# Two transformer blocks on one core: block 0's slots taken two at a time, its norms moved earlier, and block 1's last value products moved between the scores

## The chip, the cores and the metric

The kernel runs on one core of one Trainium2 chip. Its time is the device time of one launch in microseconds. All arithmetic is in float32. A core has a matrix engine (PE, with its weight loads PEld), a vector engine (DVE), a scalar engine (ACT), GpSimd (POOL) and a queue that issues DMAs (SP). Each engine works through its own list of instructions in order and waits on semaphores for the others.

## The reference, cut to what matters

A batch has 8 sequences of 512 rows and 256 columns. Two transformer blocks follow each other. Block 0 (heads of 16 columns) is

```
h = modulate(ln(x), shift_sa, scale_sa)
q, k, v = ln(heads(h))*qn_w+qn_b, ln(heads(h))*kn_w+kn_b, heads(h)   # 16 heads, 16 columns each
x = x + gate_sa * unheads(softmax(q k^T / 4) v)                      # self-attention, 512 x 512
h = modulate(ln(x), shift_ca, scale_ca)
x = x + gate_ca * (attention(h wq, kv wk, kv wv) @ ca_out_w.T + b)   # cross-attention, 64 keys
h = modulate(ln(x), shift_ff, scale_ff)
x = x + gate_ff * ((silu(h w1) * (h w3)) @ w2)                       # feed-forward, 1024 wide
```

Block 1 (heads of 64 columns, rotary positions) has self-attention, cross-attention on the same 64 context rows and a GELU feed-forward. Rows of different sequences never meet, so the eight sequences can be at different stages at one time.

## The kernel before, in words

**Everything stays on the chip.** The rows of all eight sequences (`xs[b]`) lie in the on-chip memory from start to end. The order of instructions on PE, DVE, ACT and POOL is written out by hand: inside `manual_schedule` each engine gets its instructions in the order in which the Python code emits them. DMAs go out from SP.

**Block 0 is a row of slots.** A cycle has 18 slots (`CYCLE`); sequence `b` does self-attention in cycle `b`, cross-attention in cycle `b + 1` and the feed-forward in cycle `b + 2`. So in a cycle three sequences are at work. A slot holds at most one attention block:

- a *score* part: PE multiplies keys with queries for four heads into two PSUM tiles `ps_S` of two banks each, and ACT takes the exponential of each tile into `p` (line L574, or L696 in cross-attention). There are only two such tiles, so the next score part waits until both exponentials are done;
- a *value* part: PE multiplies `p` with the values into the bank `ps_O`. In a cross-attention block it does that and also sums `p`, into two general banks.

Sixteen slots of a cycle are self-attention (four groups `g` of four heads, four key tiles `kt` each); the slots `X0` and `X1` are the two cross-attention blocks of the sequence before. A third kind of work, *others*, is put beside the slots with `at(slot, fn)`: norms, transposes, projections, the feed-forward. Functions for the same slot run in the order of their `at` calls: first all of `batch1` (self-attention) by sequence, then the keys of block 1 (`keys1`), then for each sequence `batch2` (cross-attention) and `batch3` (feed-forward). `later` holds calls that come last in their slot.

**`run_blocks` orders a slot.** It emits the scores of slot `i`, then the values of slot `i - 1`, then the others of slot `i`.

**Names that matter below.**

- `norm(n)`, n = 0 to 2: the row norm before self-attention, in pieces: statistics of row tiles 0 and 1, of tiles 2 and 3 with the power -1/2 on POOL (L175), and the application (L208), after which POOL scales and shifts.
- `head_centre`, `head_var`, `head_scale`: the norm of each head, for halves `c` of the columns; `head_scale` has the long power on POOL (L545).
- `queries_keys(g)`: four transposes (L554), then ACT makes `q` (L557) and DVE `k` (L558).
- `group_end(g)`, `group_back(g)`: the attention result leaves `ps_O` (L587), is transposed back (L596), divided by its sums (L601 to L603), and after the last group gated and added to `xs[b]` on POOL (L608, L609).
- in `batch2` and `batch3`, `prepare(n)` is the same three pieces of a norm into `z`, a buffer that both share; `turn` transposes `z` (L416) into `hT` (L417); `queries(c)` and `up(f)` multiply `hT` with weights; `down(t)` multiplies the hidden layer with `w_2` for one tile of 128 rows and, every second tile, `add_gated` takes two tiles out of PSUM (L460, L462).
- `bank_x()` hands out three general PSUM banks in turn (names `ps_X`, `ps_X`, `ps_D`).

**Block 1's self-attention** has its own slots of two blocks: scores of an odd block `i`, other jobs, scores of `i + 1`, values of `i - 1`, values of `i`. For its last sequence there are few other jobs left.

Of the kernel before, what the change touches and what calls it, by code (L numbers as in the profile page):

```python
# [22 lines left out]
DX = D + HD0  # L23
NPAIR = H // 2
# [19 lines left out]
class Block:  # L44


    def __init__(self, scores, values):
        self.scores, self.values = scores, values
        self.before, self.after = [], []


def run_blocks(blocks, beside=None):


    beside = dict(beside or {})
    for fn in beside.pop(-1, []):
        fn()
    early, late = {}, {}
    for i, bl in enumerate(blocks):
        for lead, fn in bl.before:  # L60
            early.setdefault(max(i - lead, 0), []).append(fn)
        for lag, fn in bl.after:
            late.setdefault(i + 1 + lag, []).append(fn)
    i = 0
    while i <= len(blocks) or any(k >= i for k in (*late, *beside)):
        for fn in early.get(i, []):
            fn()
        if i < len(blocks):
            for fn in blocks[i].scores:
                fn()  # L70
        if 1 <= i <= len(blocks):
            for fn in blocks[i - 1].values:
                fn()
        for fn in (*late.get(i, []), *beside.get(i, [])):
            fn()
        i += 1


def fast_path(ctx: ExitStack, tc: tile.TileContext, a: dict, out: bass.AP):
# [150 lines left out]

    sp_stack = ExitStack()
# [56 lines left out]
    nc.gpsimd.memset(hs[0][:, :, :, HD0 : HD0 + 1], 1.0)  # L288
    nc.gpsimd.memset(sc32, 0.0)
# [189 lines left out]
    X0, X1 = 9, 13  # L479


    def batch1(b):
# [8 lines left out]
        def norm(n):  # L491

            if n == 0:
                s["bc"] = bc = wk.tile([P, 3 * D], F32, tag="bc", name="bc")
                s["h"] = hs[b % 2]
                s["hv"] = s["h"][:, :, :, 0:HD0]
                s["ln"] = wk.tile([P, NT, D], F32, tag="ln", name="ln", bufs=1)
                s["pieces"] = norm_pieces(lambda: s["ln"], xs[b], EPS0)
                if b:
                    spread(bc, b, SH_SA, 3 * D)  # L500
            s["pieces"][n]()
            if b and n == 2:
                ln, bc = s["ln"], s["bc"]
                nc.gpsimd.tensor_tensor(ln, ln, bc[:, None, D : 2 * D].to_broadcast([P, NT, D]), ALU.mult)
                shift = bc[:, 0:D].rearrange("p (h d) -> p h d", d=HD0)
                nc.gpsimd.tensor_tensor(s["hv"], ln.rearrange("p t (h d) -> p t h d", d=HD0),
                                        shift[:, None].to_broadcast([P, NT, H, HD0]), ALU.add)
# [11 lines left out]
        def head_rows():  # L519
            s["z"] = wk.tile([P, NT, DX], F32, tag="zx", name="zx", bufs=1)  # L520
            nc.gpsimd.memset(s["z"][:, :, D if b else 0 : DX], 0.0)

        def head_centre(c, par=None):

            hv = s["hv"][:, :, 8 * c : 8 * c + 8] if par is None else s["hv"][:, :, 8 * c + par : 8 * c + 8 : 2]
            sh = [P, NT, hv.shape[2]]
            mean = small.tile(sh, F32, tag=f"mean{sh[2]}", name="mean", bufs=2)
            nc.vector.tensor_reduce(mean, hv, AX.X, ALU.add)
            nc.vector.tensor_scalar_mul(mean, mean, 1.0 / HD0)
            nc.vector.tensor_tensor(parts(s["z"][:, :, 0:D], c, par), hv,  # L530
                                    mean[:, :, :, None].to_broadcast([*sh, HD0]), ALU.subtract)

        def head_var(c, par=None):
            sq, z = parts(s["ln"], c, par), parts(s["z"][:, :, 0:D], c, par)
            sh = [P, NT, z.shape[2]]
            nc.scalar.activation(sq, z, AF.Square)
            s["var", c, par] = var = small.tile(sh, F32, tag=f"var{sh[2]}", name="var", bufs=2)
            nc.vector.tensor_reduce(var, sq, AX.X, ALU.add)
            nc.vector.tensor_scalar(var, var, 1.0 / HD0, EPS0, ALU.mult, ALU.add)

        def head_scale(c, par=None, eng=None):
            var, z = s["var", c, par], parts(s["z"][:, :, 0:D], c, par)
            n = z.shape[2]
            half = mhalf[:, 0 : NT * n].rearrange("p (t h) -> p t h", t=NT)
            nc.gpsimd.tensor_tensor(var, var, half, ALU.pow)  # L545
            (eng or nc.gpsimd).tensor_tensor(z, z, var[:, :, :, None].to_broadcast([P, NT, n, HD0]), ALU.mult)

        def queries_keys(g):
# [3 lines left out]
            lo = c * P + par * HD0  # L552
            for t in range(NT):
                nc.tensor.transpose(ps[:, t * P : (t + 1) * P], s["z"][:, t, lo : lo + P], ident)  # L554
# [6 lines left out]
        def block(g, kt):  # L561
# [4 lines left out]
            def score():  # L566
# [5 lines left out]
                for u in range(2):  # L572
                    pr[u] = wk.tile([P, 2, N], F32, tag="p", name="p", bufs=4)
# [11 lines left out]
        def group_end(g):  # L585
            oT = wk.tile([P, N], F32, tag="oT", name="oT")
# [3 lines left out]
        def group_back(g):  # L590
            c, par = divmod(g, 2)
            if g == 0:
                s["attn"] = wk.tile([P, NT, D], F32, tag="tok", name="attn", bufs=1)
# [3 lines left out]
            o = s["attn"][:, :, c * P : (c + 1) * P].rearrange("p t (j e d) -> p t j e d", j=4, e=2)[:, :, :, par, :]  # L597
# [5 lines left out]
            nc.vector.tensor_tensor(o, i[:, :, :, 0:HD0], inv[:, :, :, None].to_broadcast([P, NT, 4, HD0]), ALU.mult)  # L603
            check(inv.rearrange("p t j -> p (t j)"))
            if g == 3:
                at_, x = s["attn"], xs[b]
                gate = s["bc"][:, None, 2 * D : 3 * D].to_broadcast([P, NT, D])
                nc.gpsimd.tensor_tensor(at_, at_, gate, ALU.mult)  # L608
                nc.gpsimd.tensor_tensor(x, x, at_, ALU.add)  # L609

        n = 0
        for g in range(4):
            for kt in range(NT):
# [4 lines left out]
                if g == 0 and kt == 0:  # L618
                    if b == 0:
                        def before():  # L620
                            head_rows()
# [3 lines left out]
                            first_modulated(0, 0)  # L625
                            head_centre(0, 0)
                            head_var(0, 0)
                            head_scale(0, 0, nc.vector)

                        def gate():  # L630
                            spread(s["bc"][:, 2 * D : 3 * D], b, G_SA, D)
# [3 lines left out]
                        at(0, lambda: first_modulated(0, 1))  # L635
                        at(0, lambda: head_centre(0, 1))
                        at(1, lambda: head_var(0, 1))
                        at(1, lambda: head_scale(0, 1))
                        at(2, lambda: first_modulated(1))
                        at(3, lambda: head_centre(1))  # L640
                        at(4, lambda: head_var(1))
                        at(4, lambda: head_scale(1))
                        at(5, gate)
                    else:
                        for m in range(3):
                            at(i - 11 + m, lambda m=m: norm(m))
                        at(i - 6, head_rows)
                        for c in range(2):
                            at(i - 6, lambda c=c: head_centre(c))
                            at(i - 5, lambda c=c: head_var(c))  # L650
                            at(i - 4, lambda c=c: head_scale(c))
                if kt == 0:
                    at(i - 2, lambda g=g: queries_keys(g))
                if kt == NT - 1:
                    at(i + 1, lambda g=g: group_end(g))
                    at(i + 2, lambda g=g: group_back(g))
# [3 lines left out]
    def batch2(b):  # L660
# [27 lines left out]
        def block(c):  # L688
            def score():
# [4 lines left out]
                for u in range(2):  # L694
                    s["p", c, u] = p = wk.tile([P, 2, N], F32, tag="p", name="p", bufs=4)
# [35 lines left out]
        for n in range(3):  # L731
            at(base + 3 + n, lambda n=n: prepare(n))
# [12 lines left out]
    def batch3(b):  # L745
        s = {}

        base = CYCLE * (b + 2) + (3 if b in (B - 3, B - 2) else -2 if b == B - 1 else 0)
# [28 lines left out]
        def down(t):  # L777
            qp, j = divmod(t, 2)
            if j == 0:
                s["ps"] = bank_x()  # L780
            project_tile(s["ps"], j, lambda k: s["hid"][:, k, :], w_2, 8, t)
            if j == 1:
                add_gated(wk2, b, s["gate"])(qp, s["ps"].rearrange("p (j d) -> p j d", j=2))

        for n, i in enumerate((5, 5, 5) if b == B - 1 else (4, 5, 7)):
            at(base + i, lambda n=n: prepare(n))
        later.append((base + 7, turn))
        for f in range(8):
            at(base + 8 + f, lambda f=f: up(f))
        for t in range(4):  # L790
            at(base + 16 + t, lambda t=t: down(t))
# [58 lines left out]
    def keys1(p):  # L850
# [3 lines left out]
        kv1[p] = q = kv1["pool"].tile([P, N], F32, tag="q", name="q", bufs=5)  # L854
# [47 lines left out]
    for p in range(NPAIR):  # L902
        at(CYCLE + 4 + p, lambda p=p: keys1(p))
        at(CYCLE + 8 + p, lambda p=p: store_keys1(p))
# [10 lines left out]
    run_blocks(blocks, beside)  # L915
# [37 lines left out]
    with tc.tile_pool(name="ph4", bufs=2) as wk:  # L953
# [171 lines left out]
        def slots():  # L1125
            n = B * NG * NT
            for m in range(-1, n // 2):

                i = 2 * m + 1
                if i >= 0:  # L1130
                    todo[i // 16][0](i % 16 // NT, i % NT)
                jobs = steps.get(m, [])[:]
                if m in mid:
                    jobs.insert(1, mid[m])
                for fn in jobs:
# [3 lines left out]
                for k in (i - 1, i):  # L1139
# [1108 lines left out]
```

## The time and the profile before

| | |
|---|---|
| median of 3 runs | 2444.23 us (2443.59 to 2446.45) |
| the profiled execution: its own time | 2446.33 us |
| its span, first to last instruction | 2444.5 us |
| block 0: first scores to the first projections of block 1 | about 20 to 865 us |
| a full cycle (cycles 3 to 6) | 97.67 us each |
| after the last value part of cycle 7 | 731 to 865 us, feed-forward and cross-attention of the last sequences |
| block 1's self-attention, its cross-attention and feed-forward | to about 1838 us, to the end |
| PE busy, DVE, ACT, POOL | 98%, 47%, 36%, 39% of the span |

The page gives the busy time of each engine, the span in 40 slices, the DMA queues, the chain that ended last and the costliest groups. The timeline lists instructions in order of time, with neighbours of one kind merged. A merged row has its start, its length, the engine, the line, what it writes and reads, the rows and columns of the PE array and the number of instructions. A float32 matrix product appears as two instructions. The length of a PE row includes a modelled end, so distances between starts are the better measure.

### The profile page before, as it was taken

How to read it: one execution, taken by the hardware profiler on the slowest of the kernel's cores; microseconds unless marked ns; L12 is line 12 of the kernel's file. 1: busy time of each engine (PE TensorE's matmuls, PEld its weight loads, DVE VectorE, ACT ScalarE, POOL GpSimd, SP SyncE). 2: the span in 40 equal slices, each digit the busy share in tenths (PEclk: the TensorE clock that was granted, in tenths of full speed). 3: DMA queues.
4: the chain of work that ended last, by engine and by line, in shares of the span. 5: the costliest groups of instructions: out<-in, count | busy, mean ns of one | idle time of the engine just before them, and what ended most of it. 6: DMA issues, size and time to landing. Idle time of an engine off the chain costs nothing.

```text
span 2444.5 us, 28454 instructions
## 1 busy us (share of the span) xinstructions
PE 2400.8 (98%) x10964; PEld 1144.0 (47%) x10964; DVE 1147.0 (47%) x2083; ACT 887.0 (36%) x1118; POOL 955.7 (39%) x538
## 2 busy tenths in 40 slices
PE   9999999999998999999999999999999999999998
PEld 4333443444435543444444444444435555567665
DVE  4554435434434436464646454545444756651210
ACT  4565545545452123333333333333332221222221
POOL 3543222322301036555555555555543544531110
PEclk9999999999999999999999999999999999999999
DMA  5120000000001100000000000000123222210000
GB/s 181 45 93 7 16 20 8 17 11 12 13 11 55 36 1 23 19 19 19 19 18 19 18 19 18 19 18 19 36 60 98 67 68 67 63 55 27 22 18 23
DMA packets 84400, 84.07 MB, mean 34 GB/s; under 512 B 42544, under 2 KB 58784, under 8 KB 84256
## 3 DMA queue, kind: packets, MB, share of 16 engines
q1 hardware_dynamic: 83352, 81.09, 10.6%
q8 instruction: 88, 1.44, 0.2%
q10 hardware_dynamic: 904, 1.07, 0.2%
q14 instruction: 56, 0.46, 0.1%
HBM read 72.09 MB, written 10.04 MB: 34 GB/s over the span
## 4 chain that ended last, share of the span: by engine, by line
PE 88%; DVE 4%; POOL 3%; issue 2%; DMA 1%; ACT 1%; SPq 1%; POOLq 0%; DVEq 0%; ACTq 0%
PE ps_X L109 37%; PE ps_S L109 22%; PE ps_D L109 13%; PE ps_O L109 13%; PE ps_X L416 1%; DMA rb<-rec 1%; POOL x L437 1%; DMA rec<-rec 1%; DVE t L836 1%; POOL p L1260 1%; POOL q L991 1%; POOL oT L1073 1%; ACT p L574 0%; SPq L1253 0%; PE ps_X L554 0%
## 5 line engine op out<-in xcount | busy, mean ns | idle before, releaser
L109 PE MATMUL ps_S<-q,k 32*128 32x512 f32 (+1 forms) x3072 | 423.6, 624 | 8.1 <-ACT p L574 3.1
L1008 ACT ACTIVATE p<-ps_S 128x1024 f32<-128x1024 f32 x256 | 250.6, 1022 | 461.8 <-PE ps_S L109 452.0
L574 ACT ACTIVATE p<-ps_S 128x1024 f32<-128x1024 f32 x256 | 248.1, 1021 | 231.9 <-PE ps_S L109 230.5
L109 PEld LDWEIGHTS ps_S<-q,k 32*128 32x128 f32 (+1 forms) x3072 | 142.4, 184 | 242.0 <-issue 170.2
L1027 DVE TENSOR_TENSOR sm<-sm,p 128x1024 f32<-128x1024 f32 x128 | 253.2, 2037 | 2.2 <-ACT p L1008 2.2
L987 DVE TENSOR_TENSOR t<-ps_X,rope_c 128x512 f32<-128x512 f32 x126 | 87.0, 690 | 340.9 <-PE ps_X L109 340.9
L175 POOL TENSOR_TENSOR rstd<-rstd,mhalf 128x4 f32<-128x4 f32 x49 | 51.1, 1042 | 325.6 <-DVE rstd L174 324.8
L990 POOL TENSOR_TENSOR q<-t 128x512 f32<-128x512 f32 x32 | 65.5, 2047 | 288.3 <-DVE t L988 288.3
L837 POOL TENSOR_TENSOR q<-t,t 128x512 f32<-128x512 f32 x72 | 94.5, 1312 | 176.4 <-DVE t L836 170.2
L109 PE MATMUL ps_X<-hT,w 128*128 128x512 f32 x344 | 160.5, 601 | 1.4 <-ACT hT L417 0.9
L1023 POOL TENSOR_TENSOR sm<-p 128x1024 f32<-128x1024 f32 x64 | 149.9, 2369 | 3.6 <-ACT p L1008 3.6
L109 PE MATMUL ps_O<-p,h 128*32 128x512 f32 x1024 | 138.9, 613 | 1.6 <-ACT oT L587 1.6
L1073 POOL TENSOR_TENSOR oT<-oT,rb 128x512 f32<-128x512 f32 x63 | 130.8, 2093 | 18.1 <-DMA rb<-rec_d 18.1
L109 PE MATMUL ps_O<-p,v 128*64 128x512 f32 x512 | 134.8, 605 | 0.0
L109 PE MATMUL ps_D<-p,v 128*64 128x512 f32 x512 | 131.6, 592 | 0.0
L109 PE MATMUL ps_X<-w_sa_wv,hT 128*128 128x512 f32 x256 | 118.0, 604 | 0.0
L990 POOL TENSOR_TENSOR k<-t 128x512 f32<-128x512 f32 x32 | 40.8, 1275 | 194.7 <-DVE t L988 187.5
L545 POOL TENSOR_TENSOR var<-var,mhalf 128x32 f32<-128x32 f32 (+1 forms) x17 | 87.3, 5133 | 75.5 <-ACT t L773 41.7
L109 PE MATMUL ps_X<-hT,w_sa_wq 128*128 128x512 f32 x256 | 115.9, 595 | 0.0
L109 PE MATMUL ps_X<-w_sa_wo,oT 128*128 128x256 f32 x512 | 114.5, 382 | 0.1
L109 PE MATMUL ps_X<-hT,w_sa_wk 128*128 128x512 f32 x248 | 114.6, 605 | 0.0
L109 PE MATMUL ps_S<-hT,w_ff_w 128*128 128x512 f32 x256 | 111.3, 593 | 0.0
(282 smaller groups left out, 3589.3 us busy)
## 6 DMA issues: line engine op xcount, KB each, us to landing
rb<-rec SPq DMA_DIRECT2D x128, 128.0 KB
rb<-rec_d SPq DMA_DIRECT2D x124, 128.0 KB
rb<-rec SPq DMA_DIRECT2D x16, 256.0 KB
out_dram<-x SPq DMA_DIRECT2D x15, 256.0 KB
x<-in_x_dram SPq DMA_DIRECT2D x7, 512.0 KB
bc<-modd SPq DMA_DIRECT2D x7, 384.0 KB
gate<-modd SPq DMA_DIRECT2D x16, 128.0 KB
k_d<-q SPq DMA_DIRECT2D x8, 256.0 KB
```

The source lines that it names most:

```text
L109: nc.tensor.matmul(o, lhsT, rhs, start=start, stop=stop)
L175: nc.gpsimd.tensor_tensor(r[:, :n], r[:, :n], mhalf[:, :n], ALU.pow)
L416: nc.tensor.transpose(ps[:, t * P : (t + 1) * P], z[:, t, k * P : (k + 1) * P], ident)
L545: nc.gpsimd.tensor_tensor(var, var, half, ALU.pow)
L574: nc.scalar.activation(pr[u], pss[u], AF.Exp, scale=HD0 ** -0.5)
L837: nc.gpsimd.tensor_tensor(dst, t1, t2, ALU.add)
L987: nc.vector.tensor_tensor(c, ps, rope_c, ALU.mult)
L990: nc.gpsimd.tensor_tensor(r[0], ec, os, ALU.subtract)
L1008: nc.scalar.activation(pr, pss[u], AF.Exp, scale=HD1 ** -0.5)
L1023: nc.gpsimd.tensor_tensor(sm, s["p", g, 0, u], s["p", g, 1, u], ALU.add)
L1027: nc.vector.tensor_tensor(s["sm", g, u], s["sm", g, u], s["p", g, t, u], ALU.add)
L1073: eng.tensor_tensor(o, o, s["rb", g, u], ALU.mult)
```

## The change

Block 0 from slot 18 on is emitted in groups of two slots. For odd `i` the order becomes: scores of `i`, others of `i - 2`, others of `i - 1`, scores of `i + 1`, values of `i - 1`, values of `i`. The first cycle keeps the old order. With that:

- `X0` moves from slot 9 to 11, so that a group of heads ends in an odd slot or ahead of a cross-attention block;
- `queries_keys` comes four slots ahead of its scores and not two; `norm` of the next sequence comes at 13, 12 and 10 slots ahead (before: 11, 10, 9), behind cross-attention's first two norm pieces; the head norms are spread over slots -9 to -3;
- the head norms write into two kept tiles `zs[c]` (set to zero once) in place of one tile per sequence;
- each group is gated and added to `xs[b]` by itself, in place of all four at the end; `gate` and `bc` are separate DMAs;
- cross-attention's `prepare` comes in slots 3, 3, 5 (before 3, 4, 5; the last sequence 3, 3, 4); the feed-forward's in 4, 4, 7 (before 4, 5, 7), `turn` in 8, `up` from 9, `down` in every second slot from 17 for sequences 0 to 5; each `down` has a PSUM bank and two DVE instructions of its own;
- the key projections of block 1 in cycle 1 are spread over 12 slots; `p` has six buffers in place of four, other buffers have fewer.

In the last three slots of block 1's self-attention, the values of block `i - 1` come between the two score parts.

```diff
-    while i <= len(blocks) or any(k >= i for k in (*late, *beside)):
...
+    others(-1)
+    for i in range(alone):
+        scores(i)
+        values(i - 1)
+        others(i)
+    scores(alone)
+    values(alone - 1)
+    for i in range(alone + 1, max(len(blocks) + 2, *(k + 3 for k in beside)), 2):
+        scores(i)
+        if i > alone + 1:
+            others(i - 2)
+        others(i - 1)
+        scores(i + 1)
+        values(i - 1)
+        values(i)
...
-    X0, X1 = 9, 13
+    X0, X1 = 11, 13
...
+            x, gate = (v.rearrange("p t (h d) -> p t h d", d=HD0)[:, :, 8 * c + par : 8 * c + 8 : 2]
+                       for v in (xs[b], s["gate"][:, None, :]))
...
-            if g == 3:
-                at_, x = s["attn"], xs[b]
-                gate = s["bc"][:, None, 2 * D : 3 * D].to_broadcast([P, NT, D])
-                nc.gpsimd.tensor_tensor(at_, at_, gate, ALU.mult)
-                nc.gpsimd.tensor_tensor(x, x, at_, ALU.add)
+            nc.gpsimd.tensor_tensor(attn, attn, gate.to_broadcast([P, NT, 4, HD0]), ALU.mult)
+            nc.gpsimd.tensor_tensor(x, x, attn, ALU.add)
...
-                        for m in range(3):
-                            at(i - 11 + m, lambda m=m: norm(m))
-                        at(i - 6, head_rows)
+                        for m, k in enumerate((-11, -10, -9) if b == 1 else (-13, -12, -10)):
+                            at(i + k, lambda m=m: norm(m))
                         for c in range(2):
-                            at(i - 6, lambda c=c: head_centre(c))
-                            at(i - 5, lambda c=c: head_var(c))
-                            at(i - 4, lambda c=c: head_scale(c))
+                            for k, fn in zip((-6, -5, -5, -4) if b == 1 else (-7, -5, -3, -3) if c else (-9, -8, -7, -7),
+                                             (head_centre, head_square, head_var, head_scale)):
+                                at(i + k, lambda c=c, fn=fn: fn(c))
                 if kt == 0:
-                    at(i - 2, lambda g=g: queries_keys(g))
+                    at(i - (2 if i <= CYCLE else 4), lambda g=g: queries_keys(g))
                 if kt == NT - 1:
                     at(i + 1, lambda g=g: group_end(g))
-                    at(i + 2, lambda g=g: group_back(g))
+                    at(i + 2 + (b > 0 and n % 2 == 0), lambda g=g: group_back(g))
...
-        for n in range(3):
-            at(base + 3 + n, lambda n=n: prepare(n))
+        for n, i in enumerate((3, 3, 4 if b == B - 1 else 5)):
+            at(base + i, lambda n=n: prepare(n))
...
-        base = CYCLE * (b + 2) + (3 if b in (B - 3, B - 2) else -2 if b == B - 1 else 0)
+        base = CYCLE * (b + 2) + {B - 3: 4, B - 2: 3, B - 1: -2}.get(b, 0)
...
+            ps = bank_x()[:, 0:D]
+            project_tile(ps, 0, lambda k: s["hid"][:, k, :], w_2, 8, t)
+            tmp = wk2.tile([P, 2, D], F32, tag="tmp", name="tmp", bufs=1)[:, 0, :]
+            nc.vector.tensor_tensor(tmp, ps, s["gate"], ALU.mult)
+            x = xs[b][:, t, :]
+            nc.vector.tensor_tensor(x, x, tmp, ALU.add)
+
+        places = {B - 2: (3, 3, 5, 6, 8), B - 1: (5, 5, 5, 7, 8)}.get(b, (4, 4, 7, 8, 9))
...
-            at(base + 8 + f, lambda f=f: up(f))
+            at(base + places[4] + f, lambda f=f: up(f))
         for t in range(4):
-            at(base + 16 + t, lambda t=t: down(t))
+            at(base + places[4] + 8 + (t if b > B - 3 else 2 * t), lambda t=t: down(t))
...
-        at(CYCLE + 4 + p, lambda p=p: keys1(p))
-        at(CYCLE + 8 + p, lambda p=p: store_keys1(p))
+        at(CYCLE + 4 + 5 * p // 3, lambda p=p: keys1(p))
+        at(CYCLE + 7 + 5 * p // 3, lambda p=p: store_keys1(p))
...
+                end = m > n // 2 - 4
...
+                if end:
+                    todo[-1][1](2 * m % 16 // NT, 2 * m % NT)
                 for fn in jobs:
                     fn()
                 if i + 1 < n:
                     todo[(i + 1) // 16][0]((i + 1) % 16 // NT, (i + 1) % NT)
-                for k in (i - 1, i):
+                for k in (i - 1, i)[end:]:
```

## The prediction

> **What bounds the kernel now.** I read the page first: the engines' shares and the chain that ended last.
>
> ```profile
> PE 2400.8 (98%) x10964; PEld 1144.0 (47%) x10964; DVE 1147.0 (47%) x2083; ACT 887.0 (36%) x1118; POOL 955.7 (39%) x538
> ...
> PE 88%; DVE 4%; POOL 3%; issue 2%; DMA 1%; ACT 1%; SPq 1%; POOLq 0%; DVEq 0%; ACTq 0%
> ```
>
> PE is the bound, so the change can only pay in what PE loses between products. For that I read PE's timeline by starts: a dense slot first, then two slots without other work on PE.
>
> ```profile
> 405.60 1.14 PE L109 MATMUL ps_S<-q,k 16*128 16x512 f32 x8
> 406.67 1.06 PE L109 MATMUL ps_O<-p,h 128*32 128x512 f32 x8
> 407.66 1.98 PE L109 MATMUL ps_X<-hT,w 128*128 128x512 f32 x4
> 409.48 1.88 PE L109 MATMUL ps_D<-hT,w 128*128 128x512 f32 x4
> 411.29 1.14 PE L109 MATMUL ps_S<-q,k 16*128 16x512 f32 x8
> ...
> 465.88 1.14 PE L109 MATMUL ps_S<-q,k 16*128 16x512 f32 x8
> 466.95 1.06 PE L109 MATMUL ps_O<-p,h 128*32 128x512 f32 x8
> 468.19 2.04 PE L109 MATMUL ps_S<-q,k 16*128 16x512 f32 x8 [0.17 <-ACT p L574]
> 470.16 1.07 PE L109 MATMUL ps_O<-p,h 128*32 128x512 f32 x8
> 471.16 1.39 PE L109 MATMUL ps_S<-q,k 16*128 16x512 f32 x8
> ```
>
> Scores take 1.07 us, values 1.00, the eight products of an `up` 3.63, though single ones follow each other every 0.429 (8 x 0.429 = 3.43): 0.20 goes to the changes of shape. Start by start a change costs about 0.1 on each side: after values the first full product starts 0.543 later, not 0.43; scores' second group 0.534 behind the first. Within one shape 0.43 holds. In the second stretch the scores wait for the exponentials: their first half starts 1.24 after the values' start, their second 0.92 later, at **2.155**.
>
> [...] DVE's timeline has the program's order:
>
> ```profile
> 376.49 0.17 DVE L601 COPY den<-ps_D 128x16 f32<-128x16 f32 x1 [3.87 <-PE ps_D L596]
> 376.70 0.25 DVE L602 RECIPROCAL inv<-den 128x16 f32<-128x16 f32 x1
> 376.99 0.42 DVE L603 TENSOR_TENSOR attn<-ps_D,inv 128x256 f32<-128x256 f32 x1
> 377.33 0.23 DVE L146 TENSOR_REDUCE chk<-inv 128x1 f32<-128x16 f32 x2
> 377.48 0.74 DVE L199 BATCH_NORM_STATS2 st<-x 128x6 f32<-128x256 f32 x2
> ...
> 378.55 1.37 DVE L208 TENSOR_SCALAR z<-x,mv,rstd 128x256 f32<-128x256 f32 x4
> ```
>
> `group_back` (1.0), statistics (0.95), application (1.37): z is ready 4.1 us after the slot's transposes began, and the transposes of `turn` wait for it, here 0.4.
>
> **Part 1, groups of two slots (gain).** Old, two dense slots: 2 x (1.07 + 1.00 + 0.20) + F, F the other products. New: two scores 2.14, others F + 0.20, two value parts in one shape 0.454 + 2 x 0.43 + 0.543 = 1.86: 4.20 + F. That saves 0.34. But the values' 1.86 must cover the exponentials' 2.155, so the second half of the next scores comes 0.30 late, except behind the two cross-attention blocks, whose values are 0.855 longer. F of the nine pairs in a full cycle, from 0.109 a transpose, 0.429 and 0.216 a product of 512 and 256: 3.9, 7.35, 3.9, 4.8, 4.3, 7.7, 6.9, 7.3, 7.3 = 53.4. All exceed the 2.2 that cover the exponentials of the first scores, so no light slots remain. A cycle: 9 x 4.20 + 53.4 + 1.71 + 7 x 0.30 = **95.0**, against 97.67 measured (of which 1.7 is waiting of the light slots): 2.65 less.
>
> **Part 2, what is late next (loss).** Others of slots 5 and 6 now follow each other with nothing between. PE: `group_back`, the last `down`, `turn`. DVE, in `at` order: `group_back`, the next norm's statistics, the two instructions that take `down` out of PSUM, only then cross-attention's `prepare(2)`, whose z `turn` needs. From the last product of `down`: 0.42 until DVE starts (as L460 does), 0.45 and 0.35 for the two (L603's 0.424 for 256 columns from PSUM, half of L462's 0.69), 1.37 for z, 0.6 for the remaining transposes: 3.2, against 1.15 without a wait. PE stalls **2.0** in cycles 3 to 7. In cycle 2, without a `down`, z is ready at 4.3, `turn` could begin at 0.6: 3.4 of stall. In cycle 1 key rotations (2.1 of DVE) stand ahead too: 3.8. Behind PE's wait are queued the scores of `i + 1`, both value parts and, through the exponentials, ACT.
>
> **Sum by stretches**, slot for slot at equal work.
> - Cycle 1 (71.55): fewer changes, `queries_keys` earlier (scores waited 1.6 for L558 once), but light pairs and the 3.8: 0.8 less.
> - Cycle 2 (95.55): same sums with 3.4: 1.6 less.
> - Cycles 3 to 6: 97.67 - 95.0 - 2.05 = 0.6 each, 2.5.
> - Cycle 7 and the tail to 865: PE needs some 120 of the tail's 134, so 13 is waiting, 4.7 of it one gap before L416 at 752. With `down` of sequence 5 in slots 3, 5, 7, 9 that gap shrinks to about 2.2 (statistics 1.9, power 1.25 and z behind a `down` eviction, against one `down` of 3.45 on PE). But pairs of slots 9 to 12 in cycle 7 have F of 0.9 (1.07 late each), and `turn` in slot 23 waits 2.1, since per-tile evictions put the norm behind a `down`: 4.4 less.
> - Block 1's last three slots: the row for 16 scores and 32 scores there shows waits of 2.35 and 0.9 for exponentials; 1.87 of values between covers most, but the last sums wait for DVE's additions (two of them 3.44): 1.6 less.
>
> Total 10.9 less. **The clock takes some back**: nine stalls of 2 us and more[...]. By the phase of the window I count the two long ones and one of the rest: three windows at half speed, 1.7 each, 5.1 more. In all -5.8, rounded to **-6**.
>
> **Costed at nothing.** POOL: two instructions of 2.35 per sequence become eight of 256 columns, about 0.6 each (L546's 256 columns: 0.617), 5.0 for 4.7, with POOL 39% busy; if it were late, the next norm would be. DVE gets 4 x 0.8 for 2 x 1.4 per `down` set. The long power (5.43) begins three slots earlier and `queries_keys` two, with 7 us or more between; in cycle 1 I allow 0.5. `queries_keys` only needs the two `q` and `k` buffers whose scores are over. SP: one more DMA of 128 KB per sequence (`gate`), issued in 0.3 with slots to spare; key stores are later by up to 5 slots, feed-forward weights then land some 10 us later, with over 25 left before `up`. Zeroing `zs` takes about the 0.99 that L521 took at 2.5 us; POOL is next needed at 7.3. Six `p` buffers are what three blocks in flight need. If one of these covers fails, it adds to the loss side only; together I bound them by 0 and 8 us.
>
> **Profiled and plain time.** The sum is made against the profiled execution (span 2444.5, own time 2446.33), 2.1 above the median. I apply the difference to the median: 2444.2 - 6 = 2438.
>
> **The rivals.**
> - *The stall is not there*, since z's pieces get ready ahead of the eviction: then 5 x 2.0 + 3.4 + 3.8 come back and no clock is lost: -28, 2416. For it: cycle 4 before has only 0.4. Against: DVE's order above.
> - *Gains and waits cancel*: DVE is slower beside POOL (z took 2.23 for four at 381.88, L462 2.15 at 362.93, against 1.37 and 0.69). With 1 us more in each of seven cycles: +1, 2445, no change to be seen.
> - *The clock decides* (slower): the wait in front of L416 in slot 6 makes a window idle enough each time, and a second follows, as here:
>
> ```profile
> 750.00:754.60 4.60, 2.68 (x13) 2.02 (x11) 1.85 (x4) 0.00 (x0) 0.00 (x0) 1.00 0.01 4
> 754.60:761.50 6.90, 4.27 (x11) 2.41 (x12) 3.24 (x12) 1.55 (x2) 4.06 (x3) 0.52 0.06 17
> ```
>
>   (window; PE, PEld, DVE, ACT and POOL busy; then the clock: 1.00, then 0.52.) Thirteen windows at 1.7 are 22, so +11, 2455. It decides from 6.4 windows on (10.9 / 1.7). [...]
> - That groups are not formed is excluded by the loop itself.
>
> **How the numbers follow.** 0.2% of 2444 is 4.9 us, about what a measurement of this kernel can tell from no change. Forecast, chance 0.50, its own range 2430 to 2443: faster 0.35, same 0.15. No stall: 0.12, faster. Cancelling: 0.17, same 0.14, slower 0.03. Clock: 0.21, slower 0.20, same 0.01. Together faster 0.47, same 0.30, slower 0.23. The range 2419 to 2456 leaves out the far ends of the first and last rival; it takes in the 8 us of covers.
>
> **What would show it.** Pairs of value parts 1.86 long followed by scores of 1.37, not 1.07. In cycles 3 to 6, a wait of PE for z (L208) of about 2 us in front of cross-attention's transposes, once a cycle, 3.4 and 3.8 in cycles 2 and 1; cycles of about 97. The gap at 752 cut to half. If cycles last 95, the stall is absent; over 98, the clock or DVE's contention is seen in PE's granted clock or in longer rows of z. Wrong as a whole if PE waits anew somewhere not listed here.

## The result and the profile after

The changed kernel takes **2467.95 us** (2466.44 to 2469.52) beside 2444.63 us: 23 us more, a ratio of 1.0095 with an interval of 1.0077 to 1.0112. The profiled execution has a span of 2464.3 us at an own time of 2466.44, so spans can be compared with each other (2464.3 against 2444.5, +19.8).

The page of the changed kernel, its line of busy times and the shares of the chain that ended last:

```profile
PE 2406.5 (98%) x10964; PEld 1163.9 (47%) x10964; DVE 1151.4 (47%) x2115; ACT 889.8 (36%) x1118; POOL 961.8 (39%) x580
...
PE 86%; DVE 4%; POOL 3%; issue 3%; DMA 1%; ACT 1%; SPq 0%; POOLq 0%; DVEq 0%; ACTq 0%
```

PE issues as many products as before and is still the bound. It is "busy" 5.7 us longer with them, so some products take longer; the timelines below show which. The stretches are read from the trace by the start of the first scores of each cycle, and by the first products of block 1:

| profiled execution, us | before | after |
|---|---|---|
| cycle 1 | 71.55 | 80.67 |
| cycle 2 | 95.54 | 100.19 |
| cycles 3, 4, 5, 6 | 97.67 each | 97.47, 100.40, 97.47, 100.40 |
| cycle 7 and the tail, to block 1 | 221.7 | 225.0 |
| block 1's self-attention | 972.8 | 970.9 |
| half clock between 85 us and the end of block 1's self-attention | 17 | 55 |

Two `down` calls (6.9 us) have moved from cycle 2 to later, so at equal work cycle 2 is 11.6 longer and the stretch of cycle 7 is 3.6 shorter.

Cycle 4 shows the wait that was forecast. PE's timeline around cross-attention's transposes (start, length, line, what it writes and reads, idle time before it):

```profile
402.33 1.30 PE L427 MATMUL ps_D<-ident,z 128*128 128x128 f32 x4 [1.30 <-DVE z L215]
...
404.27 2.09 PE L116 MATMUL ps_S<-q,k 16*128 16x512 f32 x8
406.29 3.64 PE L116 MATMUL ps_O<-p,h 128*32 128x512 f32 x16
```

and DVE's timeline for the same time:

```profile
401.07 0.42 DVE L786 TENSOR_TENSOR tmp<-ps_X,gate 128x256 f32<-128x256 f32 x1 [1.45 <-PE ps_X L116]
401.53 0.42 DVE L788 TENSOR_TENSOR x<-x,tmp 128x256 f32<-128x256 f32 x1
401.87 1.38 DVE L215 TENSOR_SCALAR z<-x,mv,rstd 128x256 f32<-128x256 f32 x4
```

DVE takes `down` out of PSUM in two instructions and only then makes z, in the order that the prediction worked out. But look at the two PE rows behind the wait: scores last 2.09, not 1.14, and sixteen value products 3.64, not 1.92. PE runs at half speed, at a granted clock of 0.50 (403.66 to 407.08 below).

From 85 us to the end of block 1's self-attention the stretches at half clock in this trace begin at 93.05, 99.88, 120.36, 181.80, 205.69, 403.66, 601.64 and 966.86 us, always a whole number of 3.413 us apart, and last one, two or three times as long. In the trace of before they begin at 157.53 and 754.86, 175 times 3.413 apart, and last 10.24 and 6.83. So a trace can be cut at these borders into windows of 3.41 us. The table (us; busy PE, PEld, DVE, ACT, POOL with counts; then the granted clock, the share of the DMA engines and GB/s) has the windows with the waits of cycles 3, 4 and 7, and the one behind cycle 4's:

```profile
301.26:304.68 3.42, 2.30 (x11) 1.69 (x9) 1.94 (x8) 0.00 (x0) 2.23 (x4) 1.00 0.00 0
400.25:403.66 3.41, 2.11 (x10) 1.13 (x9) 2.56 (x8) 0.00 (x0) 1.06 (x3) 1.00 0.10 30
403.66:407.08 3.42, 3.42 (x16) 0.99 (x18) 3.36 (x8) 2.11 (x3) 3.32 (x2) 0.50 0.05 15
697.21:700.62 3.41, 2.11 (x11) 1.53 (x9) 1.26 (x4) 0.00 (x0) 1.85 (x3) 1.00 0.00 0
```

The wait is 1.3 us each time, and PE is busy for 2.30, 2.11 and 2.11 us, but only behind cycle 4's window does the clock fall, for two windows. So busy time alone does not decide. What differs is the work: in cycles 3 and 7 the window holds 2.30 and 2.08 us of `down` products, in cycle 4 only 0.78 of them and 1.33 of transposes. The fall is the 2.93 between cycles 3 and 4. It comes again in cycle 6 (0.67 of `down`, 1.45 of transposes) and not in cycle 5 (2.19 of `down`).

Cycle 2 shows a wait that was not forecast. PE's waits between 80 and 210 us (for what, us in total, times, longest), the forecast ones for z of cycles 1 and 2 among them:

```profile
PE ps_D L116 <- DVE oT L734: 8.0, 1, 8.0
PE ps_X L427 <- DVE z L215: 7.3, 4, 3.8
```

The 8.0 us are cross-attention's output projection (`project_out`), which waits for `scaled` (L734), which waits for the DMA of `rb`. The queue of SP and POOL's and DVE's timelines say why:

```profile
175.19 0.31 SPq L865 DMA_DIRECT2D k_d<-q  x1
175.60 0.38 SPq L729 DMA_DIRECT2D rec<-rec  x1
177.27 0.39 SPq L262 DMA_DIRECT2D w<-in_w1T_dram  x1
177.76 0.62 SPq L731 DMA_DIRECT2D rb<-rec  x1
```
```profile
167.33 5.44 POOL L561 TENSOR_TENSOR var<-var,mhalf 128x32 f32<-128x32 f32 x1
...
173.87 1.29 POOL L843 TENSOR_TENSOR q<-t,t 128x512 f32<-128x512 f32 x1
```
```profile
169.72 0.34 DVE L726 RECIPROCAL rec<-rec 128x32 f32<-128x32 f32 x1
...
185.03 0.69 DVE L734 TENSOR_TENSOR oT<-oT,rb 128x512 f32<-128x512 f32 x1 [10.47 <-DMA rb<-rec]
```

The last key of block 1 is emitted behind the long power on POOL (5.44), so its sum is done at 175.2. Its store heads SP's queue, and the reciprocals, ready at 170.1, go out only at 175.60. Then their `rb` is under way for 7 us, among 3 MB of feed-forward weights, which are loaded as soon as that last store is through.

### The profile page after: what moved, and what is told of

It reads as the page before. It is cut to its first block, busy times and chain, and to the rows that moved or that the text cites. A ratio compares the mean times of both kernels' runs of the same rounds, so it can differ in the third digit from the quotient of the medians.

```text
span 2464.3 us, 28541 instructions
## 1 busy us (share of the span) xinstructions
PE 2406.5 (98%) x10964; PEld 1163.9 (47%) x10964; DVE 1151.4 (47%) x2115; ACT 889.8 (36%) x1118; POOL 961.8 (39%) x580
## 4 chain that ended last, share of the span: by engine, by line
PE 86%; DVE 4%; POOL 3%; issue 3%; DMA 1%; ACT 1%; SPq 0%; POOLq 0%; DVEq 0%; ACTq 0%
PE ps_X L116 35%; PE ps_S L116 22%; PE ps_O L116 13%; PE ps_D L116 13%; PE ps_X L427 1%; DMA rb<-rec 1%; POOL x L448 1%; DVE t L842 1%; DVE z L215 1%; POOL p L1270 1%; ACT p L590 0%; PE ps_X L610 0%; POOL q L997 0%; POOL var L561 0%; POOL oT L1079 0%
## 5 line engine op out<-in xcount | busy, mean ns | idle before, releaser
L116 PE MATMUL ps_S<-q,k 32*128 32x512 f32 (+1 forms) x3072 | 430.9, 632 | 5.6 <-ACT p L590 3.4
L116 PEld LDWEIGHTS ps_S<-q,k 32*128 32x128 f32 (+1 forms) x3072 | 149.5, 187 | 249.7 <-issue 164.5
L116 PE MATMUL ps_X<-hT,w 128*128 128x512 f32 x328 | 151.0, 597 | 0.5 <-DVE t L779 0.5
L621 POOL TENSOR_TENSOR attn<-attn,gate 128x256 f32<-128x256 f32 x32 | 23.2, 727 | 261.6 <-DVE attn L619 255.9
```

The source lines that it names most:

```text
L116: nc.tensor.matmul(o, lhsT, rhs, start=start, stop=stop)
```

## The experiments

**Theory:** the gains of groups and tail are there; the loss is (1) half clock, started by short waits, (2) the 8.0 us for `rb`, (3) the forecast waits for z. **Rivals:** groups themselves are slow where little other work lies between; the clock is a mere by-product of the waits.

| kernel | median us | ratio to the kernel before, run beside it; interval |
|---|---|---|
| changed | 2467.95 | 1.0095, 1.0077 to 1.0112 |
| e_prep | 2433.66 | 0.9951, 0.9939 to 0.9964 |
| e_fill | 2461.35 | 1.0062, 1.0047 to 1.0078 |
| e_clock | 2468.68 | 1.0085, 1.0071 to 1.0100 |
| e_clock2 | 2450.64 | 1.0022, 1.0012 to 1.0032 |
| e_keys | 2464.06 | 1.0085, 1.0062 to 1.0108 |
| e_ff | 2466.41 | 1.0077, 1.0048 to 1.0106 |
| e_k32 | 2458.47 | 1.0050, 1.0035 to 1.0065 |
| e_third | 2457.36 | 1.0049, 1.0030 to 1.0068 |
| e_nogroups | 2457.06 | 1.0048, 1.0032 to 1.0063 |
| e_b_end | 2442.32 | 0.9984, 0.9977 to 0.9992 |
| c_prep_keys | 2435.36 | 0.9970, 0.9957 to 0.9982 |
| c_prep_k32 | 2432.56 | 0.9945, 0.9930 to 0.9959 |
| c_fill | 2431.35 | 0.9941, 0.9928 to 0.9954 |
| c_hold | 2431.05 | 0.9943, 0.9929 to 0.9956 |
| c_hold_fill | 2425.14 | 0.9906, 0.9889 to 0.9922 |

Cycle lengths below come from each kernel's one profiled execution (for e_keys, c_prep_keys and c_hold their fastest, for c_hold_fill its slowest).

### The wait for z (e_prep)

```diff
-        for n, i in enumerate((3, 3, 4 if b == B - 1 else 5)):
+        for n, i in enumerate((3, 3, 4)):
```

> The changed kernel, with the third norm piece of cross-attention one slot earlier (slot 4 in place of 5 for every sequence), so that it is emitted a group ahead of its transposes. Theory (waits for z in slot 6, and half-clock windows that follow from them): waits of 1.5 in cycles 3 to 7, 3 and 3.8 in cycles 2 and 1 go, and the stretches at half clock at 120, 205, 403 and 601 us: 18 to 26 us less, 2442 to 2450; cycles 4 and 6 last as long as 3 and 5. Rival (the clock falls for another reason): 12 to 14 less, 2454 to 2456, with cycles 4 and 6 still 3 us longer. Rival (the wait only moves to another instruction of DVE): 0 to 3 less.

34 us less than the changed kernel, more than the 18 to 26 of the theory. PE's timeline at the same place of a steady cycle, and DVE's z:

```profile
375.42 3.62 PE L116 MATMUL ps_X<-w,hid 128*128 128x256 f32 x16
378.87 0.60 PE L427 MATMUL ps_D<-ident,z 128*128 128x128 f32 x4
...
379.84 1.14 PE L116 MATMUL ps_S<-q,k 16*128 16x512 f32 x8
```
```profile
375.69 1.38 DVE L215 TENSOR_SCALAR z<-x,mv,rstd 128x256 f32<-128x256 f32 x4
```

z is ready at 377.1, under `down`'s products, and the transposes follow them without a gap. Cycles 3 to 6 are 95.30 each, where the prediction's sum without a stall was 95.0. So the wait costs 97.47 - 95.30 = 2.17 a cycle, and half clock 2.93 more in every second one. Cycle 1 falls from 80.67 to 66.28: 3.8 of that is the wait there; the rest is put down to the half clock, of which none is left between 85 and 158 us. The wait for `rb` is still 6.5.

### Clock and waiting taken apart (e_fill, e_clock, e_clock2)

e_fill makes PE work while it waits for z, e_clock also in the wait for `rb` and in five pairs with little other work. e_clock2 is e_clock with products of half the width:

```diff
         def turn():
+            ps = bank_x()
+            for _ in range({0: 8, 1: 6}.get(b, 3)):
+                mm(ps[:, 0:D], ident, w_q0[:, 0, :])     # e_fill, e_clock: all 512 columns
             s["hT"] = transposed(wk2, s["z"], b, modT[:, 2:4, :], modT[:, 0:2, :])
...
+    for i in (0, 2, 16, 18, 22):
+        at(CYCLE + i, fill)                              # 3 products; not in e_fill
+    at(2 * CYCLE + 1, lambda: fill(17))                  # not in e_fill
```

> The changed kernel, with products of constants put in front of cross-attention's transposes, into a bank that nobody reads: 3 of 0.43 us where the wait is 1.5, 6 and 8 of them in cycles 2 and 1. The waits for z stay as they are, only PE is busy in them. Theory (cycles 4 and 6 lose 2.9 each to the clock, not to the wait itself): all four steady cycles last 97.5, the stretches at 120, 205, 403 and 601 us are gone, 8 to 14 us less, 2454 to 2460. Rival (the clock follows something other than PE's activity, or the added products cost time themselves): cycles 4 and 6 stay at 100.4, 2468 or more.

> The changed kernel, with all its waits left, but with products of constants in them: those before cross-attention's transposes, 17 before the first output projection of cross-attention in cycle 2 (where the wait is 8.0) and three in each of five light pairs. Theory (the clock is more than half of the loss): no half-clock time between 85 and 800 us, 2450 to 2456. Rival (the waits are the loss, the clock a small part): 2459 to 2464.

> The changed kernel, with all its waits left and with products of constants in them as in the kernel before this one, but half as wide: 3 of 0.43 us before cross-attention's transposes in cycles 3 to 7, 6 and 8 in cycles 2 and 1, 17 before the first output projection of cycle 2, three in each of five light pairs. Theory (the clock costs more than the waits): no half-clock time between 85 and 800 us, cycles 3 to 6 of 97.5 each, cycle 1 at 71 to 74, cycle 2 at 95 to 100; 2450 to 2456. Rival (what the clock gives is lost again, since the waits end at times that POOL and the DMAs set): 2459 or more.

In e_fill all four steady cycles last 97.87 to 97.88: the 2.93 is gone from cycles 4 and 6, with the wait left. The granted clock there is 1.00, for 0.97 in cycles 4 and 6 of the changed kernel, and nothing but PE's activity was added. Products of 512 columns took 0.86, though, twice what I had written (two instructions of 0.43). So e_fill has 0.41 too much in each cycle, and its 6.6 us less fall short of the 8 to 14 expected: its cycle 2 has six windows at half clock and takes 104.5. And e_clock, with 17 of them (14.6 us) in a wait of 8.0, lost again what it won: half clock gone (mean clock 0.997 for 0.987), time unchanged. By its number the theory failed there, and e_clock decides nothing. e_clock2 has the intended size. Its windows for cycles 3 and 4:

```profile
252.90:350.40 97.50, 97.23 (x511) 46.45 (x510) 45.55 (x123) 50.57 (x62) 29.83 (x20) 1.00 0.05 14
350.40:447.90 97.50, 97.23 (x511) 46.47 (x510) 43.77 (x111) 50.58 (x62) 29.81 (x20) 1.00 0.05 14
```

Both are 97.5 long at a clock of 1.00. Cycle 1 takes 73.83, cycle 2 95.82. Only one window at half clock is left between 85 us and the end of block 1's self-attention, and the median is **17.3 us below the changed kernel**, with nothing moved and no wait taken away. So half clock makes some 17 us of the changed kernel's time, and the rival that it is a by-product falls: it has a price of its own. With the waits for z (five of 2.17, 3.8 and 2.8) that makes 34.7, near the 34 of e_prep; only near, since e_prep keeps four slow windows. Not all of the 17 is new: the kernel before has 17 us at half clock itself.

### The wait for rb (e_keys, e_ff, e_k32)

```diff
-        at(CYCLE + 4 + 5 * p // 3, lambda p=p: keys1(p))
-        at(CYCLE + 7 + 5 * p // 3, lambda p=p: store_keys1(p))
+        at(CYCLE + 4 + p, lambda p=p: keys1(p))              # e_keys
+        at(CYCLE + 8 + p, lambda p=p: store_keys1(p))
+        at(CYCLE + 4 + 3 * p // 2, lambda p=p: keys1(p))     # e_k32
+        at(CYCLE + 7 + 3 * p // 2, lambda p=p: store_keys1(p))
...
-    at(2 * CYCLE, open_ff)
+    at(2 * CYCLE + 3, open_ff)                               # e_ff, with the next line in it
+            nc.vector.memset(w[:, 0, 0:1], 0.0)
```

> The changed kernel, with block 1's keys projected one slot after the other again and stored in slots 8 to 15 of cycle 1. Theory (the last store of a key stands in SP's queue ahead of cross-attention's second reciprocals, which then travel together with the feed-forward weights): the 8.0 us wait in cycle 2 goes, and with it part of the half-clock stretch at 182 us: 8 to 10 us less, 2458 to 2460. Rival (the wait is only the collision with 3 MB of weights, wherever they stand): at most 3 less, 2465 to 2468, and the wait appears at the transfer of the first head instead.

> The changed kernel, with the feed-forward weights held back (by a small memset three slots later) until cross-attention's second reciprocals are on their way; the key stores stay. Theory (two parts: 5.5 us behind the key store in SP's queue, 3.7 us of slower transfer beside the weights): the wait of 8.0 falls to 4 to 5, 3 to 4 us less, 2464. Rival (weights alone): 8 less, 2460. Rival (queue alone): no change, 2468.

> The changed kernel, with the last two keys of block 1 one and two slots earlier (keys in every slot 3p/2 in place of 5p/3), so that the last rotation's addition on POOL stands ahead of the power of 5.4 us and not behind it. Theory (the last key's store holds up SP's queue, with cross-attention's second reciprocals behind it): the wait of 8.0 us falls to 0 to 3, 5 to 9 us less, 2459 to 2463. Rival (the weights, which then start earlier too, delay rb all the same): the wait stays over 5, above 2465.

In e_k32 PE waits no more for `rb`, and the time falls by 9.5, as the theory said, but not for its reason. Cycle 1 has 6.8 of the 9.5 (73.87 for 80.67). In cycle 2, PE from the first scores to the projection, and DVE's `scaled`:

```profile
159.69 2.10 PE L116 MATMUL ps_S<-q,k 16*128 16x512 f32 x8 [0.30 <-ACT p L590]
161.72 3.51 PE L116 MATMUL ps_O<-p,h 128*32 128x512 f32 x16
...
176.12 2.25 PE L116 MATMUL ps_D<-w_o,oT 128*128 128x256 f32 x8
```
```profile
176.06 0.69 DVE L734 TENSOR_TENSOR oT<-oT,rb 128x512 f32<-128x512 f32 x1 [5.73 <-DMA rb<-rec]
```

`rb` is there 16.4 us after the cycle's first scores, in the changed kernel 18.6: 2.2 earlier. PE gets to the projection 5.8 later, since it ran at half clock on the way. The same comparison for the others (us after the first scores of cycle 2; the last two are described below):

| | `scaled` starts | first product of the projection | wait for `rb` | half clock between |
|---|---|---|---|---|
| before | 5.6 | 8.5 | 0 | 8.1 |
| changed | 18.6 | 10.7 | 8.0 | 0 |
| e_keys | 18.5 | 16.5 | 2.2 | 10.2 |
| e_ff | 16.0 | 10.7 | 5.5 | 0 |
| e_k32 | 16.4 | 16.4 | 0 | 10.2 |
| c_prep_k32 | 15.7 | 11.6 | 4.3 | 0 |
| c_hold | 9.5 | 11.6 | 0 | 0 |

In e_keys `rb` comes no earlier at all. Its shorter wait is a slow PE, and cycle 2 still takes 99.2; the median falls by 4, with an interval that overlaps the changed kernel's. In e_ff, too, the time did not move measurably. So a shorter wait in a trace is not yet a gain, and neither the store nor the weights alone bring `rb` more than about 3 us forward. These kernels vary by the clock: one execution of e_keys took 2457.85 at a mean clock of 0.990, another 2471.65 at 0.984.

### Groups or the moves around them (e_third, e_nogroups, e_b_end)

```diff
-    run_blocks(blocks, beside, CYCLE)
+    run_blocks(blocks, beside, 2 * CYCLE)         # e_third
+    run_blocks(blocks, beside, len(blocks))       # e_nogroups
```

> The changed kernel, with groups from the third cycle on (slot 36) in place of the second. Theory (in cycle 1 a group without much other work leaves PE light, and the clock falls without any long wait): cycle 1 goes from 80.7 to 71 to 73 us with no half-clock stretches between 92 and 131 us; 8 us less, 2460. Rival (what was moved in cycle 1, norms and keys, makes it longer, not the groups): cycle 1 stays at 79 to 81, 2467.

> The changed kernel with no groups at all: slots one by one to the end, everything that was moved stays moved. Theory (groups put the norm's last piece, the eviction and the transposes into one stretch, so they make the wait; by themselves they save 2.4 a cycle): no wait for z in slot 6, steady cycles of 97 to 98 all alike, cycle 1 near 71; 2446 to 2452, between the changed kernel and the one with the earlier norm piece. Rival (the moved norms and keys make the loss, the groups only gain): waits for z stay, cycles of 99 to 102, above 2468.

> The kernel before with the change to block 1's last three slots alone (values between the two score parts). Theory (the cover of exponentials by values): the last slots of block 1's self-attention 26.7 to 23.2 us, 3.6 us less, ratio 0.9985. Rival (a half-clock window follows, as at 967 us in the changed kernel): 2 us less. Rival (the sums wait for DVE all the same): no change.

e_nogroups has no wait in the steady cycles, 97.26 each: against e_prep's 95.30 a group order without its wait is worth 2.0 a cycle. But it waits 9.8 for `rb`, cycle 2 is 104.7, and the total is above the kernel before and above what I expected: that wait belongs to the moved keys, not to the groups. e_third's gain of 10.6 looks like the theory's (cycle 1 at 74.2), but nearly half of it is cycle 2 (94.5), where the wait for `rb` was only 2.2. And e_prep has cycle 1 in groups at 66.3, so groups with little between them need not be slow. But they can be: four of the seven slow windows of the changed kernel's cycle 1 (at 93.05 and from 99.88 on) follow no gap on PE longer than 0.8 us. The two windows ahead of them, 89.64 to 93.05 and 96.46 to 99.88, hold 2.54 and 2.24 us of scores, 0.66 of transposes and at most 0.35 of value products. That is what a light group puts side by side. This rival is therefore right in part: light groups cost something in the changed kernel and nothing at that place in e_prep (clock 1.00 in its cycle 1). That the place of the scores in the windows decides which is my reading; no run varied it alone. e_b_end: block 1's self-attention 969.2 for 972.8, as the theory had it, and 0.16% less in all.

### Put together (c_prep_keys, c_prep_k32, c_fill, c_hold, c_hold_fill)

c_prep_keys and c_prep_k32 are e_prep with the key places of e_keys and e_k32. c_hold is c_prep_k32 with e_ff's edit. c_fill and c_hold_fill add three products to five light pairs (`fill` above), of 512 columns in c_fill, of 256 in c_hold_fill.

> Both moves together: cross-attention's third norm piece in slot 4 for every sequence, and block 1's keys projected and stored as in the kernel before. Theory: the wait of 6.5 us for rb, left in cycle 2 by the first move alone, shrinks to 0 to 2 with the stretch at half clock behind it: cycle 2 falls from 94.6 to 85 to 88, 6 to 9 us less than the first move alone: 2425 to 2428. Rival (the second move gained only in cycle 1, where the first has already taken the loss away): no less than 2431.

> The same key places together with cross-attention's third norm piece in slot 4. Theory: the wait for rb in cycle 2 (6.5 us with the norm piece alone) goes to 0 to 2 and nothing is lost in cycle 1: 5 to 8 us less than with the norm piece alone, 2426 to 2429. Rival (the last pairs of cycle 1 and the first of cycle 2 are so light that PE's clock falls there with or without the wait): 0 to 3 less, 2431 to 2434.

> The kernel with the earlier norm piece and the earlier keys, and with the feed-forward weights loaded only once cross-attention's second rb has been used (a small memset behind it on DVE). Theory (the reciprocals' write of 16 KB waits behind 2 MB of weights): it lands in 2 us, the wait of 4.3 for rb falls to 0 to 1, cycle 2 from 91.4 to 86 to 88, 3 to 5 us less: 2427 to 2430. Rival (the first pairs of cycle 2 are light, and the clock falls there in any case): cycle 2 stays above 89, 2431 to 2433.

> The kernel just before this one, with three products of constants of 0.43 us each put into five light pairs of cycles 1 and 2 (beside slots 18, 20, 34, 36 and 40), into a bank that nobody reads. Theory (light pairs alone let the clock fall): half-clock time between 85 and 200 us is gone, 3 to 6 us less than without, 2422 to 2425, and the runs lie closer together. Rival (the products cost what they last, up to 6.4 us, and the clock falls anyway): no less than without, 2428 to 2433.

> The kernel with all three mends (norm piece, keys, weights held) and three products of constants of 0.43 us in each of five light pairs of cycles 1 and 2. Theory (in some runs the clock falls in these light pairs): every run near the fastest one of the kernel without them, 2421 to 2426, at a mean clock of 0.996 or more. Rival (the clock falls later in those runs, or the products cost their own time): median 2429 to 2433, no narrower.

The first two gave nothing that can be told from e_prep: the rivals' side. c_prep_keys pays in cycle 1 (68.96 for 66.28, a wait of 2.0 behind key rotations on DVE). In c_prep_k32 PE, now at full clock until the wait, still waits 4.3 for `rb`. SP's queue:

```profile
153.12 0.39 SPq L262 DMA_DIRECT2D w<-in_w1T_dram  x1
...
156.49 0.34 SPq L729 DMA_DIRECT2D rec<-rec  x1
...
163.47 0.62 SPq L731 DMA_DIRECT2D rb<-rec  x1
```

Now the weights go first, and the 16 KB of reciprocals take 7 us until `rb`, which waits for them, can be issued. In c_hold, where the weights come later, SP's queue and PE's projection read

```profile
156.41 0.32 SPq L729 DMA_DIRECT2D rec<-rec  x1
157.87 0.62 SPq L731 DMA_DIRECT2D rb<-rec  x1
```
```profile
163.64 1.89 PE L116 MATMUL ps_D<-w_o,oT 128*128 128x256 f32 x8
```

1.5 us for the same 16 KB, no wait, and cycle 2 takes 84.93 for 91.43. So the store ahead in the queue and the weights each hide the other: with either gone `rb` comes 2.2 to 2.9 us earlier, with both gone 9.1. In the medians, where the theory had 2427 to 2430, c_hold shows only 1.5 less than c_prep_k32, which is no measurable gain: its executions lie between 2420.27 at a clock of 0.997 and 2435.24 at 0.991, those of c_prep_k32 between 2426.98 and 2439.18. c_fill's products cost what they gave: cycle 1 is 5.1 longer than without. With half of them c_hold_fill takes **2425.14** (2420.14 to 2428.61, clocks of 0.995 to 0.998): closer together than c_hold in only four executions, 0.9% below the kernel before, 43 us below the changed one. It is the fastest of all.

## Why the prediction was wrong

It said 2438 with a range to 2456; 2468 came. Step by step:

- **Part 1 was right.** The pair model and its cycle of 95.0 met 95.30 where the wait is gone.
- **Part 2 was right in mechanism and size.** 2.17 for 2.05 in steady cycles, 3.8 for 3.8 in cycle 1, 2.8 for 3.4 in cycle 2; the cause was DVE's order as written.
- **The other sums were near.** At equal work cycle 7 and the tail gave 3.6 less (forecast 4.4), block 1's end 3.6 in e_b_end (forecast 1.6; half clock at 967 us took half of it back in the changed kernel). The gap of 4.7 at 752 us is gone; the longest wait for z behind it is 1.5 (forecast 2.2).
- **The clock was the step that failed most.** For it "three windows at half speed, 1.7 each, 5.1 more" stood in the sum, on top of the kernel before. There were 16 (55 us) where the kernel before has 5 (17 us): eleven more. The price was about right: with the new last slots, block 1's self-attention lasts 969.2 to 969.3 in the eight runs without a slow window and 970.9 to 971.0 in the eight with one; e_clock2, with fifteen fewer and products of its own, has a span 18.1 shorter, some 1.2 a window. So the term was 13 to 19 us, by my estimate from these two prices, and not 5.1. The choice of three out of nine stalls was my estimate, made at a single phase of the windows, and not shown by the trace of before. There half clock follows windows with PE busy for 1.84 us (154.12 to 157.53) and 1.23 (751.45 to 754.86), but not one with 1.84 (51.72 to 55.13). In cycle 4 of the changed kernel it followed a wait of 1.3. I had also counted PE only as busy or idle, so that the windows before 93.05 and 99.88, with PE busy for 3.40 and 2.83 us in scores, transposes and few value products, were not in the count. The rival "the clock decides" had 13 windows and the right sign; it lacked the next point.
- **A cover failed.** "Feed-forward weights then land some 10 us later, with over 25 left before `up`" asked only who waits for the weights. It did not ask what stands behind the key store in SP's queue, nor who shares the transfer: `rb` was there 18.6 us after cycle 2's first scores, before 5.6, and PE waited 8.0 us, at the upper bound of 8 that I had given all covers together. The prediction named the power on POOL and the later key stores in one paragraph and did not put the two together.

The remainder: -10.9, 8.0 and 13 to 19 make 10 to 16 of the 19.8 between the spans. In e_clock2, which has nearly no half clock, cycles 3 to 6 last 0.4 longer each than the sum said, and cycle 1 takes 73.83 where 71.55 - 0.8 was forecast; its added products and one slow window are in that. The rest of the difference stays open.

## What to carry to other kernels

When work is merged into larger groups, look at what the vector engine must finish between the last product of a group and the first product that needs its result, and move that one piece a whole group ahead: here one slot's difference was worth 34 us, about half of it wait and half the clock behind it. Price a wait of the bound engine twice, once for itself and once for the clock (2.17 and 2.93 us in cycle 4 here). Take the windows of the trace (3.41 us here, by the borders of its half-clock stretches) at every phase, with what PE does in them and not only whether it is busy. For each transfer that is moved, ask what is queued behind it and what shares its time, not only when its own data are needed. And compare the time at which the data arrive, not only the wait for them, which also shrinks when the waiting engine is slow (e_keys: wait 2.2 for 8.0 us, data at 18.5 for 18.6).

## What the runs showed of the hardware that was not expected

- The clock fell behind a window with PE busy for 2.11 us (cycle 4, 400.25 to 403.66) and behind one with PE busy for 3.40 of its 3.41 (89.64 to 93.05), while it stayed at 1.00 behind a third with 2.11 (cycle 7, 697.21 to 700.62).
- The 17 traces, from 85 to 2400 us, were cut into windows at the borders of their own half-clock stretches, and a product was taken to last until the next one starts, or to its recorded end. Of 10393 windows at full clock with 1.9 us or more of products other than scores of block 0 (16 of the array's 128 rows in the views, `16*128`) and transposes, none was followed by half clock (1222 of them in the traces of before and after), though in 55 of them PE had no product for over 1 us. All ten windows with 2.0 us or more of those scores and at most 0.4 of those other products were followed by it; two of them are those before 93.05 and 99.88. No run varied the kind of product alone, so it was not shown that the kind is the cause. e_fill has the instructions of the changed kernel's cycle 1, with products of constants ahead of the transposes, and stayed at full clock there (1.00 from 85.70 to 158.10, for 0.85 from 85.80 to 166.50): its windows have at most 2.01 us of those scores, each with 0.45 or more of value products.
- One slow window cost 1.7 us in block 1's self-attention. In e_ff each steady cycle has one and lasts 98.83 beside 97.47, 1.4 more; two of them cost 2.93 in the changed kernel. With products of constants in the waits for z the clock was 1.00 in cycles 3 to 6 of e_fill and in cycles 3 and 4 of e_clock2.
- A write of 16 KB took 7.0 us until its successor could go when 2 MB had been issued ahead of it on the same queue and 1 MB just behind (c_prep_k32), and 1.5 us without them (c_hold).
